# Two small layer-norm steps on GpSimd, a selector in another buffer, and a new instruction order in a four-layer graph network kernel

## The chip, the cores and the metric

The kernel runs on one core of one Trainium2 chip. The metric is the device time of one execution in microseconds (us), smaller is better. All executions quoted here are of the undisturbed, fast state. A comparison counts as faster or slower only from 2% on. TensorE is the matrix engine, VectorE, ScalarE and GpSimd are the elementwise engines, and in profile lines they are called PE (with PEld for its weight loads), DVE, ACT and POOL.

## The reference, cut to what matters

128 graphs of 64 nodes with 512 features each go through four layers. Each layer is `x = x + layer(relu(layernorm(x)), adj)`.

```python
def _layernorm(x, axis=-1, eps=1e-5):
    m = jnp.mean(x, axis=axis, keepdims=True)
    v = jnp.var(x, axis=axis, keepdims=True)
    return (x - m) / jnp.sqrt(v + eps)
# layer 0 on h = relu(layernorm(x)):
h = jax.nn.relu(hypergraph_conv(h, adj, W1, b1))     # 512 -> 1024
h = layer_norm(h, gamma, beta)
y = hypergraph_conv(h, adj, W2, b2)                  # 1024 -> 512, then + its input
# layer 1: s = (h @ w) @ a;  A = exp(leaky(8 tanh((s_i + s_j) / 8))) * adj, rows rescaled;  A @ h @ w
# layer 2: weight = adj * exp(q k^T), rows normalised;  weight @ value
# layer 3: attention from two vectors, then three powers of the transition with Wk[0..2], relu
# ... (inputs: x 128x64x512, adj 128x64x64, weights; all float32)
```

## The kernel before: the parts that matter

The program is a list of operations, each with an engine, an estimated cost and what it reads and writes. A list scheduler lays them out in one order per engine. The order depends on the estimated costs and on a table of start offsets (`AT`), stretches and periods. Every engine then executes its own instructions in that order, and an instruction whose input is late holds up the ones behind it (the timelines of VectorE and GpSimd below show it).

```python
class Graph:
    def op(self, eng, cost, fn, r=(), w=()):   # record one operation
        ...
    def run(self, slots, after):               # lay all out, by readiness, cost and priority, then emit
        ...

STRETCH, PERIOD1, PERIOD2 = (1.62, 0.5, 2.98, 1.93), 88.03, 82.78
AT = {
    "x0": -940.38, "apart": -46.64, "w1": -1103.01, "b1": -852.79, "w2": -823.68, ...   # start
    ... "m": 23.25, "h0": -18.86, "p0": 0.21, ... "y0": -114.53, ... "e0": -274.6, ...  # layers 0 and 1
    ... "hT": -11.06, "sh": 23.19, ... "b1_": 29.67,                                    # layers 2 and 3
}
```

The 128 graphs are 16 groups of 8. The first pass takes all groups through layers 0 and 1, the second through layers 2 and 3. One group takes some 74 us in either pass, and this is called a period below.

```python
def setup_l0():
    p, row, sel = Buf("ps"), Buf("o"), Buf("tmp")       # sel holds one of the four 128x512 temporaries
    for i in range(2):
        dve(0.2, lambda i=i: nc.vector.tensor_copy(quad(sel)[0:2, i, :], ...), [], [(sel, i)])
    # ... W2's row sums on TensorE, then spread over the partitions with the selector

def norm_stats(src, k, r):
    st, mv, ve, rs = Buf("st"), Buf("mv"), Buf("ve"), Buf("rs")
    for i in range(k):
        dve(0.69, lambda i=i: nc.vector.bn_stats(st.t[:, i, :], src(i)), [r[i]], [(st, i)])
    dve(0.19, lambda: nc.vector.bn_aggr(mv.t, ...), [...], [mv])
    dve(0.15, lambda: nc.vector.tensor_scalar_add(ve.t, mv.t[:, 1:2], EPS), [mv], [ve])
    pool(0.65, lambda: nc.gpsimd.tensor_tensor(rs.t, ve.t, mhalf, ALU.pow), [ve], [rs])
    return mv, rs

def pre_stats(g, t):
    mv, rs = norm_stats(...)
    dve(0.21, lambda: nc.vector.scalar_tensor_tensor(nm.t, mv.t[:, 0:1], -1.0, rs.t, op0=ALU.mult, op1=ALU.mult), [mv, rs], [nm])
    return nm, rs

def pre_ln(g, t, stats=None):        # h = relu(x * rstd - mean * rstd), on ScalarE
    ...

def layer0(g):
    ...
            h = pre_ln(g, t)
            pool(1.43, lambda xx=xx, h=h: nc.gpsimd.tensor_add(xx.t, xx.t, h.t), [h, xx], [xx])          # wide
            pool(1.39, lambda xx=xx: nc.gpsimd.tensor_add(xx.t, xx.t, b2_b.t), [xx, b2_b], [xx])         # wide
    ...     # W1 and W2 products as seven block products each; their input combinations on VectorE:
            #   dve(c_v(kc * P), lambda: nc.vector.tensor_tensor(d(), x_(), y_(), op), ...)
            # W2's results come out of PSUM on VectorE into y, and y into the output product:
            pe(c_mm(512, 1), lambda ...: nc.tensor.matmul(pf.t, M.t[:, t, :], y.t, start=True, stop=True), ...)

def layer1(g):
    ...
        h = pre_ln(g, t, stats[t])
        dot(lambda h=h: h.t, lambda: wa_b.t, ...)        # a dot product on VectorE, line 372
    ...
```

Of the kernel before, what the change touches and what calls it, by code (L numbers as in the profile page):

```python
# [11 lines left out]
ALU = mybir.AluOpType  # L12
AX = mybir.AxisListType

P = 128
# [6 lines left out]
EPS = 1e-5  # L22
# [139 lines left out]
def tile_adj_preln_d4(  # L162
# [6 lines left out]
    nc = tc.nc  # L169
# [74 lines left out]
    def c_mm(n, count):  # L244
        return 2 * count * max(n * 2 / 2400 + 0.0025, 0.111)
# [6 lines left out]
    def pe(cost, fn, r, w):  # L252
        return G.op("PE", cost, fn, r, w)

    def dve(cost, fn, r, w):
        return G.op("DVE", cost, fn, r, w)
# [4 lines left out]
    def pool(cost, fn, r, w):  # L261
        return G.op("POOL", cost, fn, r, w)
# [4 lines left out]
    def quad(b):  # L267
        return b.t.rearrange("p (c k) -> p c k", c=4)



    STRETCH, PERIOD1, PERIOD2 = (1.62, 0.5, 2.98, 1.93), 88.03, 82.78
    AT = {
        "x0": -940.38, "apart": -46.64, "w1": -1103.01, "b1": -852.79, "w2": -823.68, "w": 75.08, "c1": -847.71,
        "l0": -445.55, "c2": -663.72, "l1": 79.9, "c": -67.88, "g0": -1126.08, "g1": -1034.6, "g2": -833.84,
        "g3": -1004.6, "g": -1141.81, "l3": 18.25, "wg": 50.45, "w3": 213.12, "last": -71.37, "load1": -95.02,
        "load2": 65.29, "m": 23.25, "h0": -18.86, "p0": 0.21, "z0": 15.08, "q0": 10.02, "y0": -114.53, "h1": -19.75,
        "p1": -10.66, "z1": -12.15, "q1": -11.04, "y1": -111.67, "s": -30.12, "t0": 8.48, "e0": -274.6, "t1": 33.65,
        "e1": -92.85, "hT": -11.06, "sh": 23.19, "lq": 8.25, "pt": -36.14, "v": -8.42, "pv": -37.45, "s3": 0.07,
        "tt": -200.64, "a0": 29.6, "b0": -28.1, "a1": 61.9, "b1_": 29.67,  # L280
    }

    def part(name):
# [138 lines left out]
    def setup_l0():  # L422


        p, row, sel = Buf("ps"), Buf("o"), Buf("tmp")
        for i in range(2):
            dve(0.2, lambda i=i: nc.vector.tensor_copy(quad(sel)[0:2, i, :], ident[0:2, i:i + 1].to_broadcast([2, P])), [], [(sel, i)])
        gsc = const.tile([P, KH, 2], F32, name="gsc")
        dve(0.2, lambda: nc.vector.tensor_scalar(gsc[:, :, 0], gb2[:, 0, :], 1.0 / DH, None, op0=ALU.mult), ["gb2g"], ["gsc0"])
        dve(0.2, lambda: nc.vector.tensor_copy(gsc[:, :, 1], gb2[:, 1, :]), ["gb2b"], ["gsc1"])  # L430
# [4 lines left out]
        pe(c_mm(512, KH), mm, ["gsc0", "gsc1", *wkeys("w2", 0, KH)], [p])  # L435
        act(0.6, lambda: nc.scalar.copy(row.t[0:2, :], p.t[0:2, :]), [p], [row])
        pm, pb = Buf("ps"), Buf("ps")
        pe(c_mm(512, 1), lambda: nc.tensor.matmul(pm.t, quad(sel)[0:2, 0, :], row.t[0:2, :], start=True, stop=True), [row, (sel, 0)], [pm])
        pe(c_mm(512, 1), lambda: nc.tensor.matmul(pb.t, quad(sel)[0:2, 1, :], row.t[0:2, :], start=True, stop=True), [row, (sel, 1)], [pb])
        act(0.6, lambda: nc.scalar.copy(bw2_b.t, pb.t), [pb], [bw2_b])  # L440
        for c in range(KH):
            dve(0.75, lambda c=c: nc.vector.scalar_tensor_tensor(
# [59 lines left out]

    def norm_stats(src, k, r):

        st, mv, ve, rs = Buf("st"), Buf("mv"), Buf("ve"), Buf("rs")
        for i in range(k):
            dve(0.69, lambda i=i: nc.vector.bn_stats(st.t[:, i, :], src(i)), [r[i]], [(st, i)])  # L507
        dve(0.19, lambda: nc.vector.bn_aggr(mv.t, st.t[:, :k, :].rearrange("p k s -> p (k s)")), [(st, i) for i in range(k)], [mv])
        dve(0.15, lambda: nc.vector.tensor_scalar_add(ve.t, mv.t[:, 1:2], EPS), [mv], [ve])  # L509
        pool(0.65, lambda: nc.gpsimd.tensor_tensor(rs.t, ve.t, mhalf, ALU.pow), [ve], [rs])  # L510
        return mv, rs

    def pre_stats(g, t):

        xx, nm = xt[g, t], Buf("nm")
        mv, rs = norm_stats(lambda i: xx.t, 1, [xx])
        dve(0.21, lambda: nc.vector.scalar_tensor_tensor(nm.t, mv.t[:, 0:1], -1.0, rs.t, op0=ALU.mult, op1=ALU.mult), [mv, rs], [nm])  # L517
        return nm, rs

    def pre_ln(g, t, stats=None):  # L520
# [480 lines left out]
    for k in range(3):  # L1001
        src = Wk3[k].rearrange("(c p) o -> p c o", p=P)
        for c in (0, 2):
            i = k * KD + c
# [69 lines left out]
```

## Time and profile before

| | before |
|---|---|
| time, median (lowest to highest), 4 runs | 2438.2 us (2436.1 to 2440.3) |
| profiled span | 2439.8 us |
| first-pass period (mean between output products of the 5th and the 14th group) | 74.29 us |
| second-pass period | 73.81 us |

The engine shares, the stretches, the start and the groups are shown and read in the prediction. Two things are needed beside them.

A float32 matmul of the program stands in the trace as two records, and a transpose on TensorE as one (5933 matmuls and 64 transposes give the 11930 records). At full pace a record of 512 columns starts 0.43 us after the one before it. Ends of matmuls are modelled in this profile. So I also count TensorE's waits from start to start: the time from one matmul's start to the next one's, less what a matmul of its width takes at full pace. I did this count fully only after the prediction. The "waits" below are this count.

The chain of work that ended last, by engine, in the kernel before:

```profile
PE 71%; DVE 14%; DMA 7%; ACT 5%; issue 3%; SPq 0%; POOL 0%; DVEq 0%; ACTq 0%
```

TensorE was busy 98% of the time, but the chain that set the end was elsewhere for 29% of it, and nearly half of that is VectorE. TensorE's own instructions are therefore often released by something else at the last moment.

The timeline of the kernel before, at a place that comes back in every first-pass period (start, length, engine, line, operation; other lines between these are left out; L586 is a combination of the W1 product's inputs on VectorE, L695 and L696 are the wide additions of h and b2 on GpSimd, L594 is here a W1 product, L624 the last evacuation of a W2 product into y, L730 the output product that reads y):

```profile
556.83 1.27 POOL L695 TENSOR_TENSOR x<-x,h 128x512 f32<-128x512 f32 x1
557.07 1.31 DVE L586 TENSOR_TENSOR s_s_vu_tt<-mT_a 128x256 f32<-128x256 f32 x1
558.18 1.33 POOL L696 TENSOR_TENSOR x<-x,row_sh_q 128x512 f32<-128x512 f32 x1
558.42 1.37 DVE L586 TENSOR_TENSOR s_s_vu_tt<-s_s_vu_tt,mT_a 128x256 f32<-128x256 f32 x1
558.50 1.88 PE L594 MATMUL ps<-wa_mem,mT_a 128*128 128x512 f32 x4
...
559.71 0.41 DVE L586 TENSOR_TENSOR mT_a<-mT_a 128x256 f32<-128x256 f32 x1
560.04 0.41 DVE L624 TENSOR_TENSOR y_qT<-ps,u 128x256 f32<-128x256 f32 x1
...
560.51 1.12 PE L730 MATMUL ps<-y_qT,bd 128*128 128x512 f32 x2
```

Two combinations of 128x256 take 1.31 and 1.37 us beside GpSimd's wide additions, where the next one takes 0.41. Each ends 0.28 us after one of the additions (558.10 and 558.38, 559.51 and 559.79). The evacuation stands behind them in VectorE's queue, and the output product starts as soon as the evacuation ends (560.04 + 0.41 = 560.45). That is a wait of TensorE, though hardly any idle time shows for it.

This place is one of several. Of the 30.4 us of waits from 244 to 1160 us, 5.2 stand before output products. W1 products have 12.1, W2 products that read ScalarE's transposed copies (rT_a) 9.4, left multiplications 3.8.

### The profile page before, as it was taken

What the parts mean: (1) busy time and instruction counts of PE and PEld (TensorE: products, weight loads), DVE (VectorE), ACT (ScalarE), POOL (GpSimd) and SP (SyncE); (2) the same over time, 40 slices, a digit from 0 to 9 for tenths busy, and PEclk for the clock granted to TensorE, in tenths of its full rate; (3) what the DMA queues carried; (4) which work ended last, traced back from release to release, by engine and by line L of the source; (5) the groups of instructions that cost most, each with busy time, mean ns of one, the idle gap of its engine ahead of it and who ended that gap; (6) DMA issues with size and microseconds to landing.
All of it is one profiled execution on the core that took longest, in us unless ns stands there. A gap on an engine that the chain in (4) does not pass through costs nothing.

```text
span 2439.8 us, 33261 instructions
## 1 busy us (share of the span) xinstructions
PE 2381.8 (98%) x11930; PEld 1851.8 (76%) x11930; DVE 1836.4 (75%) x4252; ACT 1265.6 (52%) x1754; POOL 723.3 (30%) x874
## 2 busy tenths in 40 slices
PE   7999999999999999999999999999999999999999
PEld 3576667766667766677678888888888888888887
DVE  6888988888988889887778566666676766676764
ACT  2666565666555665555645455444455444454432
POOL 3233334333344323344223222222222222222221
PEclk8999999999999999999999999999999999999999
DMA  6322232222222322313453222223222223322211
GB/s 208 81 69 53 61 74 59 76 65 53 66 60 70 78 48 57 78 54 76 104 134 59 72 59 68 50 61 72 68 59 67 56 61 72 65 62 59 50 40 42
DMA packets 335927, 168.76 MB, mean 69 GB/s; under 512 B 284689, under 2 KB 290833, under 8 KB 335761
## 3 DMA queue, kind: packets, MB, share of 16 engines
q1 hardware_dynamic: 335760, 166.63, 28.2%
q8 instruction: 94, 1.54, 0.3%
q14 instruction: 73, 0.59, 0.1%
HBM read 64.76 MB, written 34.70 MB: 41 GB/s over the span
## 4 chain that ended last, share of the span: by engine, by line
PE 71%; DVE 14%; DMA 7%; ACT 5%; issue 3%; SPq 0%; POOL 0%; DVEq 0%; ACTq 0%
PE ps L594 48%; PE ps L817 12%; PE ps L533 3%; DMA z_hT<-tmp_mB_s 3%; PE ps L935 2%; DVE s_s_vu_tt L586 2%; DVE st L507 2%; PE ps L878 2%; DMA rw<-row 1%; PE ps L730 1%; DVE nm L517 1%; ACT h L524 1%; ACT rT_a L544 1%; DVE s_s_vu_tt L868 1%; DVE x L731 1%
## 5 line engine op out<-in xcount | busy, mean ns | idle before, releaser
L524 ACT ACTIVATE h<-x,nm,rs 128x512 f32<-128x512 f32 x384 | 303.1, 811 | 541.3 <-DVE nm L517 490.2
L594 PE MATMUL ps<-wb_mem,rT_a 128*128 128x256 f32 x2056 | 477.9, 381 | 10.3 <-ACT rT_a L544 8.4
L594 PEld LDWEIGHTS ps<-wb_mem,rT_a 128*128 128x128 f32 x2056 | 387.2, 190 | 78.1 <-ACT rT_a L544 20.5
L510 POOL TENSOR_TENSOR rs<-ve,mhalf 128x1 f32<-128x1 f32 x320 | 199.2, 624 | 692.6 <-DVE ve L509 605.6
L594 PE MATMUL ps<-wb_mem,s_s_vu_tt 128*128 128x256 f32 x1152 | 275.0, 380 | 0.6 <-DVE s_s_vu_tt L586 0.6
L594 PE MATMUL ps<-wb_mem,tmp_mB_s 128*128 128x256 f32 x1152 | 261.6, 379 | 1.0 <-DVE tmp_mB_s L586 1.0
L594 PE MATMUL ps<-wa_mem,mT_a 128*128 128x512 f32 x512 | 243.0, 603 | 9.3 <-ACT u L562 7.4
L594 PE MATMUL ps<-wb_mem,mT_a 128*128 128x256 f32 x1016 | 242.7, 380 | 0.0
L594 PEld LDWEIGHTS ps<-wb_mem,tmp_mB_s 128*128 128x128 f32 x1152 | 217.5, 190 | 30.8 <-DVE tmp_mB_s L586 1.8
L594 PEld LDWEIGHTS ps<-wb_mem,s_s_vu_tt 128*128 128x128 f32 x1152 | 216.3, 190 | 31.8 <-DVE s_s_vu_tt L586 2.0
L594 PEld LDWEIGHTS ps<-wb_mem,mT_a 128*128 128x128 f32 x1016 | 189.8, 190 | 30.5 <-issue 6.0
L507 DVE BATCH_NORM_STATS2 st<-x 128x6 f32<-128x512 f32 x256 | 175.9, 687 | 28.0 <-DMA x<-xm 25.3
L594 PEld LDWEIGHTS ps<-wa_mem,mT_a 128*128 128x128 f32 x512 | 93.8, 191 | 123.8 <-issue 95.7
L948 POOL TENSOR_TENSOR u<-u,bk_b 128x256 f32<-128x256 f32 x96 | 75.7, 796 | 368.6 <-DVE x L953 215.2
L594 PE MATMUL ps<-wa_mem,s_s_vu_tt 128*128 128x512 f32 x384 | 183.0, 600 | 1.3 <-DVE z_hT L614 1.3
L562 ACT COPY u<-ps 128x256 f32<-128x256 f32 (+1 forms) x160 | 73.0, 456 | 200.0 <-PE ps L594 153.6
L544 ACT COPY rT_a<-z_hT 128x1024 uint16<-128x1024 uint16 x128 | 145.4, 1160 | 21.6 <-DMA z_hT<-tmp_mB_s 21.4
L564 DVE TENSOR_TENSOR u<-ps,u 128x256 f32<-128x256 f32 (+1 forms) x160 | 84.5, 528 | 95.6 <-PE ps L594 64.2
L533 PEld LDWEIGHTS ps<-bd,h 128*128 128x128 f32 x1024 | 129.0, 193 | 33.6 <-issue 13.6
L695 POOL TENSOR_TENSOR x<-x,h 128x512 f32<-128x512 f32 x64 | 86.2, 1346 | 194.0 <-ACT h L524 194.0
L952 DVE TENSOR_TENSOR u<-ps,u 128x256 f32<-128x256 f32 x96 | 40.6, 423 | 136.3 <-PE ps L594 121.6
L533 PE MATMUL ps<-bd,h 128*128 128x128 f32 x1024 | 132.2, 278 | 3.6 <-DVE bd L759 1.5
(172 smaller groups left out, 4248.4 us busy)
## 6 DMA issues: line engine op xcount, KB each, us to landing
x<-in_x_dram SPq DMA_DIRECT2D x64, 256.0 KB, 2.7
xm<-x SPq DMA_DIRECT2D x64, 256.0 KB, 2.0
x<-xm SPq DMA_DIRECT2D x64, 256.0 KB, 2.6
out_dram<-x SPq DMA_DIRECT2D x64, 256.0 KB, 2.2
adj<-in_adj_dram SPq DMA_DIRECT2D x32, 256.0 KB, 4.2
rw<-row SPq DMA_DIRECT2D x96, 64.0 KB, 3.2
wb_mem<-in_Wk_dram SPq DMA_DIRECT2D x6, 512.0 KB, 4.8
wa_mem<-in_W1T_dram SPq DMA_DIRECT2D x2, 1024.0 KB, 8.5
```

The lines of the kernel that those rows point to most:

```text
L507: dve(0.69, lambda i=i: nc.vector.bn_stats(st.t[:, i, :], src(i)), [r[i]], [(st, i)])
L510: pool(0.65, lambda: nc.gpsimd.tensor_tensor(rs.t, ve.t, mhalf, ALU.pow), [ve], [rs])
L524: act(0.82, lambda: nc.scalar.activation(h.t, xx.t, AF.Relu, bias=nm.t, scale=rs.t), [xx, nm, rs], [h])
L533: nc.tensor.matmul(quad(p)[:, c, :], h.t[:, c * P:(c + 1) * P], rhs(), start=True, stop=True)
L544: act(1.16, lambda: nc.scalar.copy(u16(dst()).rearrange("p c (k q) -> p c k q", q=2), u16(back()).rearrange("p (q c r) -> p c r q", q=2, c ...
L562: act(n / 1200 + 0.17, lambda: nc.scalar.copy(at(0)(), p1.t[:, :n]), [p1], [(U, 0)])
L564: dve(c_v(n), lambda: nc.vector.tensor_add(at(1)(), p2.t[:, :n], at(0)()), [p2, (U, 0)], [(U, 1)])
L586: dve(c_v(kc * P), lambda: nc.vector.tensor_tensor(d(), x_(), y_(), op), [*kx, *ky], kd)
L594: nc.tensor.matmul(p.t[:, :n], lhs()[:, c, :], rhs(c), start=first and c == 0, stop=c == kc - 1, skip_group_check=True)
L695: pool(1.43, lambda xx=xx, h=h: nc.gpsimd.tensor_add(xx.t, xx.t, h.t), [h, xx], [xx])
L817: nc.tensor.matmul(pair(p.t)[:, o, :], a, b, start=first and o == 0 and c == 0, stop=c == 1, skip_group_check=True)
L948: pool(0.88, lambda: nc.gpsimd.tensor_add(U.t[:, iv], U.t[:, u[1]], add()), [u, ka], [v])
```

## The change

The intent: take two one-column steps of every layer norm off VectorE, give the start one more temporary, and lay the order out anew for the new costs.

```diff
-    STRETCH, PERIOD1, PERIOD2 = (1.62, 0.5, 2.98, 1.93), 88.03, 82.78
+    STRETCH, PERIOD1, PERIOD2 = (2.01, 1.52, 3.8, 3.15), 99.32, 100.99
     AT = {
-        "x0": -940.38, ... "m": 23.25, "h0": -18.86, ... "y0": -114.53, ... "e0": -274.6, ...
+        "x0": -1000.31, ... "m": -52.0, "h0": -37.33, ... "y0": -29.58, ... "e0": -103.04, ...
     ...   (all entries of the table are new)
-        p, row, sel = Buf("ps"), Buf("o"), Buf("tmp")
+        p, row, sel = Buf("ps"), Buf("o"), Buf("rw")
     ...   (and the views of sel to match)
-        dve(0.15, lambda: nc.vector.tensor_scalar_add(ve.t, mv.t[:, 1:2], EPS), [mv], [ve])
-        pool(0.65, lambda: nc.gpsimd.tensor_tensor(rs.t, ve.t, mhalf, ALU.pow), [ve], [rs])
+        pool(0.3, lambda: nc.gpsimd.tensor_scalar_add(rs.t, mv.t[:, 1:2], EPS), [mv], [rs])
+        pool(0.65, lambda: nc.gpsimd.tensor_tensor(rs.t, rs.t, mhalf, ALU.pow), [rs], [rs])
     ...
-        dve(0.21, lambda: nc.vector.scalar_tensor_tensor(nm.t, mv.t[:, 0:1], -1.0, rs.t, op0=ALU.mult, op1=ALU.mult), [mv, rs], [nm])
+        pool(0.3, lambda: nc.gpsimd.tensor_scalar(nm.t, mv.t[:, 0:1], rs.t, -1.0, op0=ALU.mult, op1=ALU.mult), [mv, rs], [nm])
```

## The prediction

> **What bounds the kernel now.** I read the page's engine shares first, then busy time by stretch, then the start on the TensorE timeline, then the groups by form for every operation that the change touches.
>
> The page, by engine:
> ```profile
> PE 2381.8 (98%) x11930; PEld 1851.8 (76%) x11930; DVE 1836.4 (75%) x4252; ACT 1265.6 (52%) x1754; POOL 723.3 (30%) x874
> ```
> TensorE is busy 98% of 2439.8 us, so it sits idle for only 58.0 us. All of VectorE, ScalarE and GpSimd lies beside it. A shorter small operation on those engines is worth only what it takes away from TensorE's waits.
>
> Where those 58 us lie: busy us of each engine by stretch (columns: stretch, length, then PE, PEld, DVE, ACT, POOL busy, granted clock, DMA share, GB/s):
> ```profile
> 0.00:61.00 61.00, 44.50 (x124) 21.39 (x125) 39.78 (x82) 13.09 (x20) 22.40 (x29) 0.89 0.62 208
> ...
> 244.00:1160.00 916.00, 903.02 (x3754) 640.76 (x3753) 781.70 (x1816) 534.39 (x756) 348.64 (x403) 1.00 0.27 65
> ...
> 1400.00:2380.00 980.00, 970.61 (x5780) 832.84 (x5778) 656.39 (x1526) 459.02 (x623) 229.34 (x291) 1.00 0.27 60
> ```
> The start (0 to 61 us) has 61.00 - 44.50 = 16.5 us of idle, the steady first pass (layers 0 and 1) 13.0 us in 916, the steady second pass 9.4 us in 980. The rest, some 19 us, is the end of the setup (5 us), the passage between the two passes (9 us) and the tail (5 us). VectorE has 85% in the first pass (781.70 of 916): it is the engine next to the bound there, and it has 67% in the second.
>
> The start on TensorE's timeline (start, length, work; in brackets the idle before it and what ended it):
> ```profile
> 5.59 5.45 PE L468 MATMUL ps<-tmp_mB_s 128*128 128x512 f32 x8 [5.59 <-DMA tmp_mB_s<-in_Wk_dram]
> 15.53 3.29 PE L468 MATMUL ps<-tmp_mB_s 128*128 128x512 f32 x4 [4.49 <-DMA tmp_mB_s<-in_Wk_dram]
> ...
> 44.20 3.78 PE L594 MATMUL ps<-wa_mem,mT_a 128*128 128x512 f32 x4 [3.21 <-ACT u L562]
> 47.77 3.06 PE L594 MATMUL ps<-wa_mem,s_s_vu_tt 128*128 128x512 f32 x4
> 50.67 7.03 PE L468 MATMUL ps<-tmp_mB_s 128*128 128x512 f32 x16
> ```
> The 512-wide matmul takes 7.03 / 16 = 0.44 us at 50.67 but 3.78 / 4 = 0.94 us at 44.20, just after an idle stretch. So an idle stretch of TensorE at the start is paid twice. Taking 0.43 us as the full pace, the cold matmuls at 5.59, 15.53, 44.20 and 47.77 cost about 2.0 + 1.6 + 2.1 + 1.3 = 7 us more. Start waste: about 16.5 + 7 = 23.5 us.
>
> **What the Trainium skill says.** "TensorE: Matmul & The Clock Gate", Part 1, What's actually happening: TensorE runs at half clock until it has been busy for about 3.4 us, and falls back after an idle window of that length. The trace agrees (0.94 against 0.44 us, above). "Perfetto Trace Analysis", Identifying the Most-Contended Engine: matmul occupancy is not the distance from the roofline, weight-load busy share is better; here 76%. "SBUF — State Buffer", Practical consequences: a VectorE instruction with two SBUF inputs contends with a GpSimd instruction that reads SBUF. The trace has such spreads (the 128x1 product of line 517 has a median of 152 ns and a longest of 1266 ns). "GPSIMD Engine Reference", 3.1: GpSimd pays a larger dispatch and more cycles per element than VectorE; the rows below agree.
>
> **The change part by part.** The groups by form (count, busy us, mean ns, idle before and its cause):
> ```profile
> L509 DVE TENSOR_SCALAR ve<-mv 128x1 f32<-128x1 f32 x320 | 49.0, 153 | 10.3
> L517 DVE SCALAR_TENSOR_TENSOR nm<-mv,rs 128x1 f32<-128x1 f32 x256 | 58.0, 232 | 22.8 <-POOL rs L510 22.3 <-POOL s_s_vu_tt L858 0.3
> ...
> L510 POOL TENSOR_TENSOR rs<-ve,mhalf 128x1 f32<-128x1 f32 x320 | 199.2, 624 | 692.6 <-DVE ve L509 605.6 <-DVE nm L517 58.3 <-ACT rT_a L939 16.8
> ...
> L695 POOL TENSOR_TENSOR x<-x,h 128x512 f32<-128x512 f32 x64 | 86.2, 1346 | 194.0 <-ACT h L524 194.0
> ...
> L948 POOL TENSOR_TENSOR u<-u,bk_b 128x256 f32<-128x256 f32 x96 | 75.7, 796 | 368.6 <-DVE x L953 215.2 <-DVE u L566 152.0
> ```
> *Layer norm steps.* Removed from VectorE: 320 additions of eps at 153 ns = 49.0 us, and 256 products -mean * rstd at 232 ns = 58.0 us (the rows give the busy sums; records overlap slightly). Together 107 us, so VectorE falls from 1836 to about 1729 us, 71%. Added to GpSimd: the same 576 instructions. The fixed cost, an estimate from the rows: 128x512 takes 1346 and 128x256 takes 796, so 256 elements cost 550 ns and nothing costs about 246 ns. 576 x 0.25 = 144 us, so GpSimd goes from 723 to about 867 us, 36%. The chain bn_aggr, eps, power, product, activation loses one hand-over (VectorE to GpSimd to VectorE to ScalarE becomes VectorE to GpSimd to ScalarE), and the product no longer queues behind wide VectorE work; it gains about 0.2 us of slower arithmetic. What ends TensorE's waits in the first pass is instead the evacuations and the transposed copies (line 624 before line 730, 566 and 562 before the next W1 product, 544 before the W2 product): a layer norm does not appear among them, it is computed far ahead. So 107 us off VectorE is worth little directly: I put 2 us on it, for evacuations that find VectorE free.
>
> *Selector.* The two 2x128 copies move from one of the four temporaries to the row buffer, which nobody uses until the first attention row. In the kernel before, the selector held a temporary from 1.8 to about 41 us, so the four Wq, Wk pairs had three buffers: the second Wk is issued at 11.08, only after the first pair's matmuls, and lands at 15.40, and the fourth pair is only multiplied at 50.67. In the new order, both first pairs can be issued at once.
>
> *Order.* The instruction order of the new kernel (built, not run) has the same 5997 matmuls. The DMA queue starts with the 2 MB of W1, then two Wq, Wk pairs, then four x tiles, then adj. From the landings before, the stream goes at 0.65 us per 256 KB after some 3 us, so 3 MB land by about 10 us: TensorE starts near 9.5 instead of 5.6 (4 us later), but then runs both pairs without the 4.5 us hole, until about 20. The small products and two left multiplications follow at 20 to 25.5 (24.6 to 30.2 before), then pairs 3 and 4 (16 matmuls at 0.43 plus the bias columns, 8.7 us), then the W2 row sums (7.0 us), to about 41. Before, at 44.2, TensorE had done the same but for pairs 3 and 4 (8.7 us), and had done a W1 product and the two selector products (4 us). So the new one is 3.2 + 8.7 - 4 = about 8 us ahead, and runs warm where the old one paid 3.4 us at 44 to 50. I count 8 in all, as evacuations may open a hole of their own.
> In the steady first pass, the old period of about 74 us has some 2 us of waits of 0.1 to 0.6 us, repeated 16 times. The new period still puts a W2 product, one W1 product (0.86 us) and the output product together once, as before, but the second time a left multiplication and a W1 product more stand between them; W2 products come in runs of 12 and 16. I count 0.3 us per period, 5 us. In the second pass the weight loads and matmuls leave almost nothing: 0. The passage and tail: 0, give or take 3.
>
> Sum: 2439 - 2 - 8 - 5 = 2424 us.
>
> **Rivals.** (1) GpSimd becomes slow to deliver: three dependent small steps, queued behind 1.35 us additions in order, delay the activations. For: the power already takes 624 ns, and GpSimd and VectorE share reads. Against: 45% of GpSimd at most in the first pass, and layer norm lies ahead of need. If it did, every group would lose about 1 us, +30: 2455 to 2470. (2) The new order loses in the steady passes what it wins at the start: a hole of 0.5 us more in each of 32 periods is 16 us, so 2445. For: the order was made with a model of costs, not on this trace. (3) VectorE was the hidden limit of the first pass, and its relief removes all waits there: another 20 us, 2404. Against: TensorE's idle there is only 13 us. (4) Transfers hidden anyway: if the x tiles and not Wk limit the start, the selector brings nothing and W1 first costs 4 us: 2434.
>
> **Range and chances.** 2% is 49 us. All idle is 58 us and the cold clock 7, of which at least 10 us of the start (first weights) and the tail can't go; so faster by over 2% would need nearly everything. 2% slower would need rival 1 in full in every period. Range 2404 (rival 3) to 2443 (near rival 2).
>
> **What would show it.** Right: VectorE busy near 1730 and GpSimd near 865; TensorE busy in the first 61 us up from 44.5 to 49 or more, with the first matmul near 9.5 us and no second hole before 19; the first pass period down by some 0.3 us; the second pass equal. Wrong if activations of h end TensorE's waits, if the small GpSimd steps take over 0.4 us, or if a transition between passes opens several us.

## The result, and the profile after

| | before | after |
|---|---|---|
| median, 4 runs each | 2438.2 us | 2399.9 us (2397.0 to 2403.2) |
| ratio, 95% interval | | 0.9843 (0.9826 to 0.9860) |
| profiled span | 2439.8 us | 2395.1 us |
| first-pass period | 74.29 us | 71.77 us |
| second-pass period | 73.81 us | 73.21 us |
| first matmul starts at | 5.6 us | 9.5 us |
| waits of TensorE from there to 61 us | 20.1 us | 8.5 us |
| waits in 61 to 122 us | 3.2 us | 6.2 us |
| waits in 244 to 1160 us | 30.4 us | 2.6 us |

Here and below, a ratio is the mean time of one kernel's fast runs over that of the other kernel's fast runs of the same rounds, so it isn't quite the ratio of the medians. By the 2% rule the two kernels are the same. The time came out 24 us under the one predicted, and 4 us under the predicted range.

The page of the changed kernel, by engine:

```profile
PE 2356.3 (98%) x11930; PEld 1855.0 (77%) x11930; DVE 1721.2 (72%) x3676; ACT 1263.5 (53%) x1754; POOL 938.2 (39%) x1450
```

TensorE is still at 98%. This number, at which one would look first, says nothing about what happened. VectorE lost 115 us, GpSimd gained 215 us.

The chain that ended last, by engine, in the changed kernel:

```profile
PE 84%; DVE 6%; DMA 4%; ACT 2%; POOL 2%; issue 2%; SPq 0%; DVEq 0%; POOLq 0%; ACTq 0%
```

This line does say it: the chain runs on TensorE itself for 84% instead of 71%, and VectorE's part fell from 14% to 6%.

Busy time by stretch in the changed kernel (columns as in the prediction):

```profile
0.00:61.00 61.00, 48.81 (x170) 24.96 (x171) 44.55 (x84) 16.52 (x26) 36.66 (x54) 0.97 0.69 237
244.00:1160.00 916.00, 914.62 (x3858) 661.74 (x3857) 725.82 (x1605) 555.01 (x786) 429.62 (x665) 1.00 0.27 68
```

In the first pass TensorE's idle time fell from 13.0 to 1.4 us, and it ran 3858 matmul records in the 916 us instead of 3754. That is 2.8% more work in the same time, far more than 11.6 us of idle explain; the waits between starts explain it. The weight loads show it too: their busy time in this stretch rose from 640.76 to 661.74 us, by 3.3%, where groups came 3.5% faster.

The start of the changed kernel on TensorE's timeline:

```profile
9.52 8.34 PE L469 MATMUL ps<-tmp_mB_s 128*128 128x512 f32 x12 [9.52 <-DMA tmp_mB_s<-in_Wk_dram]
...
23.34 2.02 PE L534 MATMUL ps<-bd,h 128*128 128x128 f32 x16 [1.14 <-ACT bd L682]
26.21 7.10 PE L469 MATMUL ps<-tmp_mB_s 128*128 128x512 f32 x16 [0.84 <-DMA tmp_mB_s<-in_Wk_dram]
...
34.92 7.03 PE L435 MATMUL ps<-wb_mem,gsc 128*2 128x512 f32 x16
```

TensorE starts 3.9 us later than before, then runs to 44 us with no idle hole above 1.14 us. All four weight pairs are done at 33 us; before, the last pair was still running at 57 us.

The groups by form of the moved steps in the changed kernel (count, busy us, mean ns, idle before and its cause):

```profile
L518 POOL TENSOR_SCALAR nm<-mv,rs 128x1 f32<-128x1 f32 x256 | 119.3, 466 | 26.4
L510 POOL TENSOR_SCALAR rs<-mv 128x1 f32<-128x1 f32 x320 | 101.5, 317 | 534.2 <-DVE mv L509 452.9 <-ACT rT_a L940 43.7 <-ACT mT_a L940 16.7
```

The two steps take 317 and 466 ns on average on GpSimd where I had estimated 250, 221 us in all instead of 144. Their medians in the trace are 222 and 265 ns, and the longest 839 and 1383: most take about what was estimated, and the mean is made by those that are held up (three in ten take over 1.3 times the median). What holds them up is not in these rows.

One group of the W1 combinations on VectorE, first in the kernel before, then in the changed kernel:

```profile
L586 DVE TENSOR_TENSOR s_s_vu_tt<-s_s_vu_tt,mT_a 128x256 f32<-128x256 f32 x64 | 40.8, 638 | 2.0
```

```profile
L587 DVE TENSOR_TENSOR s_s_vu_tt<-s_s_vu_tt,mT_a 128x256 f32<-128x256 f32 x64 | 27.1, 423 | 1.7
```

The same instruction takes 423 ns instead of 638 on average, and at most 426 instead of 1376: in the new order none of them is held up. Not every group does so well: the one before it in the queue fell from 638 to 514 ns, and in f2 (below), with the same period, this one takes 505.

The place of the output product in the changed kernel's timeline (L625 is the evacuation, L595 a W1 product, L731 the output product):

```profile
581.49 0.81 DVE L625 TENSOR_TENSOR y_qT<-ps,u 128x256 f32<-128x256 f32 x2
581.61 1.88 PE L595 MATMUL ps<-wa_mem,mT_a 128*128 128x512 f32 x4
...
583.33 1.88 PE L731 MATMUL ps<-y_qT,bd 128*128 128x512 f32 x4
```

The evacuation ends at 582.30 and the output product comes at 583.33: a full microsecond of slack where before there was none. A W1 product keeps TensorE busy meanwhile, but one stood there before too (558.50). What changed is VectorE's queue: no slowed combinations stand in front of the evacuation.

The two profiled executions are 44.7 us apart. Counted from the span's start, so with the wait for the first matmul, the waits differ by stretch as follows: 0 to 61 us, 7.7 us fewer (11.6 fewer after the first matmul, which comes 3.9 later); 61 to 122, 3.0 more; 122 to 244, 4.2 fewer; 244 to 1160, 27.8 fewer; 1160 to 1400, the passage between the passes, under 1 fewer; from 1400 us on some 7 fewer (6 to 7, as one takes the full pace of the smallest matmuls). Together that is the 44.7 us to within 0.5.

### The profile page after: what moved, and what is told of

Its sections match the earlier page's. It is cut to its first block, busy times and chain, and to the rows that moved or that the text cites. A ratio compares the mean times of both kernels' runs of the same rounds, so it can differ in the third digit from the quotient of the medians.

```text
span 2395.1 us, 33543 instructions
## 1 busy us (share of the span) xinstructions
PE 2356.3 (98%) x11930; PEld 1855.0 (77%) x11930; DVE 1721.2 (72%) x3676; ACT 1263.5 (53%) x1754; POOL 938.2 (39%) x1450
## 4 chain that ended last, share of the span: by engine, by line
PE 84%; DVE 6%; DMA 4%; ACT 2%; POOL 2%; issue 2%; SPq 0%; DVEq 0%; POOLq 0%; ACTq 0%
PE ps L595 60%; PE ps L818 11%; PE ps L534 4%; PE ps L936 2%; PE ps L731 2%; PE ps L879 2%; DVE s_s_vu_tt L869 1%; DMA x<-xm 1%; PE ps L844 1%; ACT o L543 1%; DVE bd L854 1%; ACT h L525 1%; POOL u L867 1%; POOL rs L511 1%; DVE st L508 1%
## 5 line engine op out<-in xcount | busy, mean ns | idle before, releaser
L595 PE MATMUL ps<-wb_mem,rT_a 128*128 128x256 f32 x2056 | 476.8, 380 | 1.7 <-DVE z_hT L615 0.9
L595 PEld LDWEIGHTS ps<-wb_mem,rT_a 128*128 128x128 f32 x2056 | 386.5, 190 | 74.8 <-issue 20.3
L510 POOL TENSOR_SCALAR rs<-mv 128x1 f32<-128x1 f32 x320 | 101.5, 317 | 534.2 <-DVE mv L509 452.9
L595 PE MATMUL ps<-wb_mem,s_s_vu_tt 128*128 128x256 f32 x1152 | 275.0, 379 | 0.2 <-DVE s_s_vu_tt L587 0.2
L595 PE MATMUL ps<-wb_mem,tmp_mB_s 128*128 128x256 f32 x1152 | 261.3, 379 | 0.2 <-DVE tmp_mB_s L587 0.2
L595 PEld LDWEIGHTS ps<-wb_mem,s_s_vu_tt 128*128 128x128 f32 x1152 | 218.5, 190 | 43.1 <-issue 10.5
L595 PE MATMUL ps<-wb_mem,mT_a 128*128 128x256 f32 x1016 | 240.7, 380 | 1.8 <-ACT u L563 1.3
L595 PEld LDWEIGHTS ps<-wb_mem,tmp_mB_s 128*128 128x128 f32 x1152 | 217.6, 190 | 29.6 <-DVE tmp_mB_s L587 0.6
L595 PE MATMUL ps<-wa_mem,mT_a 128*128 128x512 f32 x512 | 238.0, 593 | 2.1 <-DVE u L567 2.1
L511 POOL TENSOR_TENSOR rs<-rs,mhalf 128x1 f32<-128x1 f32 x320 | 202.9, 634 | 26.6
L595 PEld LDWEIGHTS ps<-wb_mem,mT_a 128*128 128x128 f32 x1016 | 190.6, 190 | 28.6 <-ACT u L563 1.5
L595 PE MATMUL ps<-wa_mem,s_s_vu_tt 128*128 128x512 f32 x384 | 182.9, 599 | 1.0 <-ACT c_b L453 0.6
L595 PEld LDWEIGHTS ps<-wa_mem,mT_a 128*128 128x128 f32 x512 | 96.0, 190 | 105.4 <-issue 92.5
L623 POOL TENSOR_TENSOR u<-u,row_sh_q 128x256 f32<-128x256 f32 x96 | 70.9, 746 | 235.0 <-DVE u L565 205.9
L707 ACT ACTIVATE z_hT<-z_hT 128x512 f32<-128x512 f32 x128 | 79.8, 625 | 116.7 <-DVE z_hT L615 116.6
```

The costliest lines, as they stand in the source:

```text
L510: pool(0.3, lambda: nc.gpsimd.tensor_scalar_add(rs.t, mv.t[:, 1:2], EPS), [mv], [rs])
L511: pool(0.65, lambda: nc.gpsimd.tensor_tensor(rs.t, rs.t, mhalf, ALU.pow), [rs], [rs])
L595: nc.tensor.matmul(p.t[:, :n], lhs()[:, c, :], rhs(c), start=first and c == 0, stop=c == kc - 1, skip_group_check=True)
L707: act(0.63, lambda: nc.scalar.activation(z.t[:, cols], z.t[:, cols], AF.Relu), [(z, j)], [(z, j)])
```

## The experiments

My theory after reading the two traces was **order**: the new order alone lets TensorE run the first pass without waits, and where the small steps run matters little. The rival was **relief**: VectorE was the hidden limit of the first pass, and 107 us less of its work removed the waits. This is the third rival of the prediction. All times below are medians, the ratios are against the kernel before in the same rounds. The kernel before had medians of 2435.1, 2436.1, 2436.3, 2441.1 and 2441.8 us in the five sets of runs, each on another chip, so medians of different sets agree only within some 5 us and ratios are the better measure between sets.

| run | what it is | median us | ratio (95%) | first-pass period us |
|---|---|---|---|---|
| f1_old_order_gpsimd | old order, both steps on GpSimd | 2479.6 | 1.0182 (1.0167 to 1.0197) | 76.84 |
| f2_new_order_vector | new order, both steps on VectorE | 2402.3 | 0.9865 (0.9850 to 0.9879) | 71.77 |
| e1_norm_only | before plus moved steps, scheduled anew | 2494.8 | 1.0243 (1.0227 to 1.0258) | 77.12 |
| e2_order_only | before plus all new constants | 2450.7 | 1.0057 (1.0040 to 1.0074) | 74.55 |
| h1_old_start | after, old start constants | 2414.3 | 0.9913 (0.9896 to 0.9929) | 71.77 |
| h2_old_first_pass | after, old first-pass constants | 2497.3 | 1.0252 (1.0237 to 1.0268) | 77.08 |
| h3_old_second_pass | after, old second-pass constants | 2413.1 | 0.9904 (0.9888 to 0.9921) | 71.77 |
| e3_no_selector | after, selector in a temporary | 2404.9 | 0.9872 (0.9858 to 0.9887) | 71.77 |
| h5_b_new_first | before, new first-pass constants | 2417.3 | 0.9923 (0.9908 to 0.9938) | 71.77 |
| g1_no_b2 | before without the b2 additions | 2420.1 | 0.9933 (0.9918 to 0.9948) | 72.96 |
| f3_old_order_eps | old order, eps on GpSimd | 2449.7 | 1.0055 (1.0040 to 1.0070) | 75.37 |
| f4_old_order_product | old order, product on GpSimd | 2451.3 | 1.0059 (1.0042 to 1.0076) | 75.20 |
| f5_f1_no_b2 | f1 without the b2 additions | 2447.3 | 1.0028 (1.0017 to 1.0039) | 74.42 |
| d1_f2_more_vector | f2 with more work on VectorE | 2439.9 | 0.9997 (0.9988 to 1.0006) | 73.37 |
| g2_no_adds | before without both wide additions | 2418.1 | 0.9902 (0.9887 to 0.9917) | 72.89 |
| f6_f1_no_adds | f1 without both wide additions | 2432.8 | 0.9960 (0.9945 to 0.9975) | 73.26 |
| k1_product_vector | after, product on VectorE | 2397.1 | 0.9813 (0.9799 to 0.9828) | 71.77 |
| k2_eps_vector | after, eps on VectorE | 2398.9 | 0.9826 (0.9809 to 0.9842) | 71.77 |

Where differences of less than 2% are read as differences here, it is because the 95% intervals of the ratios lie apart. All gave a correct result except g2_no_adds and f6_f1_no_adds, which leave out an addition on purpose. (b2 is all zeros in these inputs, so leaving its addition out changes no result here.) By the 2% rule e1 and h2 are slower than the kernel before, k1 is unclear, and all others are the same.

Several expectations missed. f1 (2479.6) is above every case that was written down, and e1 and h2 are above theirs by 35 and 7 us. f3, f5 and h3 fell between their two cases. h5 is 2 us above its range, e2 and k1 are within 1 us outside. h1 had 13.7 us of waits in its first 61 us where 16 to 20 were expected, and g1's period fell by 1.33 us where 0.4 to 1 was. f2's VectorE was 1789 us busy, not near 1830.

### The order and the small steps, crossed

The scheduler's order depends on the engine and cost that an operation is recorded with. To keep an order exactly, the two crossed kernels keep the recorded engine and cost and change only which engine's instruction is emitted.

f1_old_order_gpsimd, from the kernel before:

```diff
-        dve(0.15, lambda: nc.vector.tensor_scalar_add(ve.t, mv.t[:, 1:2], EPS), [mv], [ve])
-        pool(0.65, lambda: nc.gpsimd.tensor_tensor(rs.t, ve.t, mhalf, ALU.pow), [ve], [rs])
+        dve(0.15, lambda: None, [mv], [ve])
+        def eps_pow():
+            nc.gpsimd.tensor_scalar_add(ve.t, mv.t[:, 1:2], EPS)
+            nc.gpsimd.tensor_tensor(rs.t, ve.t, mhalf, ALU.pow)
+        pool(0.65, eps_pow, [ve, mv], [rs])
...
-        dve(0.21, lambda: nc.vector.scalar_tensor_tensor(nm.t, ...), [mv, rs], [nm])
+        dve(0.21, lambda: nc.gpsimd.tensor_scalar(nm.t, mv.t[:, 0:1], rs.t, -1.0, op0=ALU.mult, op1=ALU.mult), [mv, rs], [nm])
```

> The order of the kernel before, matmul for matmul and operation for operation, but eps and -mean * rstd are emitted on GpSimd at the same places. Order theory (the new order alone took the first pass's waits away): the first-pass period stays near 74 us and the time at 2432 to 2440. Relief theory (VectorE's 107 us less is what took them away): the period falls to about 72 us and the time to about 2405 to 2412. Half and half: near 2420.

f2_new_order_vector, from the changed kernel:

```diff
-        pool(0.3, lambda: nc.gpsimd.tensor_scalar_add(rs.t, mv.t[:, 1:2], EPS), [mv], [rs])
+        pool(0.3, lambda: nc.vector.tensor_scalar_add(rs.t, mv.t[:, 1:2], EPS), [mv], [rs])
...
-        pool(0.3, lambda: nc.gpsimd.tensor_scalar(nm.t, ...), [mv, rs], [nm])
+        pool(0.3, lambda: nc.vector.scalar_tensor_tensor(nm.t, mv.t[:, 0:1], -1.0, rs.t, op0=ALU.mult, op1=ALU.mult), [mv, rs], [nm])
```

> The order of the changed kernel, matmul for matmul, but the two small steps are emitted on VectorE at the places where GpSimd had them. Order theory: the period stays at 71.8 us and the time at 2398 to 2405, with VectorE back near 1830 us busy. Relief theory: the period goes back to about 74 us, the time to about 2430.

Measured: f1 took 2479.6 us, 44 us more than before, and f2 took 2402.3, 33 us less than before. The stretch from 400 to 1000 us decides it. Busy time by engine in it (PE, PEld, DVE, ACT, POOL), for the kernel before:

```profile
400.00:1000.00 600.00, 591.54 (x2463) 420.07 (x2462) 512.83 (x1197) 354.51 (x501) 225.52 (x262) 1.00 0.27 66
```

for f1:

```profile
400.00:1000.00 600.00, 573.49 (x2368) 402.22 (x2367) 473.11 (x996) 339.36 (x482) 265.31 (x411) 1.00 0.25 61
```

for f2:

```profile
400.00:1000.00 600.00, 600.00 (x2526) 432.69 (x2525) 505.81 (x1231) 360.80 (x516) 243.84 (x272) 1.00 0.26 66
```

and for the changed kernel:

```profile
400.00:1000.00 600.00, 600.00 (x2525) 432.50 (x2524) 476.53 (x1057) 368.32 (x522) 281.69 (x436) 1.00 0.26 66
```

f1 has VectorE relieved (473 instead of 513 us busy), and TensorE gets less done (2368 records instead of 2463). f2 has VectorE nearly as loaded as before (506 us), and TensorE is busy for all 600 us with 2526 records, as many as the changed kernel. So the order carries the gain and the relief does not; f2 shows it directly. f1 is not relief alone, as it loads GpSimd too, and relief alone in the old order was not run. The first-pass period is 71.77 us in f2 as in the changed kernel, to the hundredth: with 1.1 and 2.6 us of waits in the 916 us from 244 on, that is TensorE's own pace for a group.

What the moved steps are worth in the new order is at the edge of what the runs tell: f2 and the changed kernel differ by 2.3 us in the medians and by 0.0022 in the ratio (some 5 us), with overlapping intervals.

### The parts as a scheduler user would try them

e1_norm_only has the new `norm_stats` and `pre_stats` of the diff above with the old constants; e2_order_only has all the new constants and nothing else.

```diff
 # e2_order_only, from the kernel before
-    STRETCH, PERIOD1, PERIOD2 = (1.62, 0.5, 2.98, 1.93), 88.03, 82.78
+    STRETCH, PERIOD1, PERIOD2 = (2.01, 1.52, 3.8, 3.15), 99.32, 100.99
     ... (and the new table)
```

> The kernel before with the new norm_stats and pre_stats alone; the constants of the order are the old ones, so that the scheduler lays out another order from the new costs (its matmul order shows no short repeating period). Order theory: constants that were fitted to other costs give an order no better than before, 2430 to 2460. Relief theory: 2405 to 2420.

> The kernel before with the new constants alone; norm steps on VectorE, selector in the temporaries. Order theory in its plain form (the constants carry the gain): 2400 to 2410. If the constants fit only the costs that they were found with: 2420 to 2450, as the first pass finds no short period. Relief theory: about 2430.

Measured: 2494.8 and 2450.7 us, both longer than before. These are not clean halves, as another engine, cost or constant gives another order. e2's period stays at 74.55 us, although f2 shows that an order with the small steps on VectorE can reach 71.77. It isn't the recorded costs that keep e2 there: h5 below has the same ones, only without the new start and second-pass constants, and reaches 71.77. Why e2 doesn't is not shown. What follows is only that neither e1 nor e2 gains.

### Which part of the order

Three kernels put back one part of the old constants, one puts back the selector's buffer, and one gives the kernel before only the new first-pass constants.

```diff
 # h1_old_start, from the changed kernel: the table's start entries
-        "x0": -1000.31, "apart": -0.04, "w1": -1140.59, ...
+        "x0": -940.38, "apart": -46.64, "w1": -1103.01, ...
```

```diff
 # h2_old_first_pass, from the changed kernel: entries of layers 0 and 1
-    STRETCH, PERIOD1, PERIOD2 = (2.01, 1.52, 3.8, 3.15), 99.32, 100.99
+    STRETCH, PERIOD1, PERIOD2 = (1.62, 0.5, 3.8, 3.15), 88.03, 100.99
     ... "load1": -95.02, "m": 23.25, ... "e1": -92.85
```

```diff
 # h3_old_second_pass, from the changed kernel: entries of layers 2 and 3
+    STRETCH, PERIOD1, PERIOD2 = (2.01, 1.52, 2.98, 1.93), 99.32, 82.78
     ... "wg": 50.45, ... "hT": -11.06, ... "b1_": 29.67
```

```diff
 # h5_b_new_first, from the kernel before: the new entries of layers 0 and 1
+    STRETCH, PERIOD1, PERIOD2 = (2.01, 1.52, 2.98, 1.93), 99.32, 82.78
     ... "load1": -120.84, "m": -52.0, ... "e1": -32.68
```

```diff
 # e3_no_selector, from the changed kernel (with the views to match)
-        p, row, sel = Buf("ps"), Buf("o"), Buf("rw")
+        p, row, sel = Buf("ps"), Buf("o"), Buf("tmp")
```

> The changed kernel with the old constants for the setup and first loads alone; after three groups its matmul order settles on the same period as the changed kernel's. If the first pass is worth about 30 us and the start about 10: the time is 2408 to 2415, the first 61 us have about 16 to 20 us of waits, the steady period 71.8 us. If the start were the larger part of the gain: 2425 or more.

> The changed kernel with the old constants of layers 0 and 1 alone (start and second pass new, small steps on GpSimd). If the first pass's order carries the gain, and GpSimd's steps cost in an order that was not fitted to them: a period of 74 to 77 us, 2440 to 2490. If GpSimd's relief carried it: near 2405.

> The changed kernel with the old constants of layers 2 and 3 alone. The second pass had only some 6 us less waiting after the change: 2400 to 2410. If the second pass and the passage between the passes mattered more than the traces say: 2415 or more.

> The kernel before (small steps on VectorE, selector in the temporaries, old start, old second pass) with the new constants of layers 0 and 1 alone. Its matmul order settles on a short period of its own that is like the changed kernel's. If longer runs between producer and use are what takes the waits away: a first-pass period of 71.8 to 72.3 us, the time 2405 to 2415. If the exact order of the changed kernel is needed: 2425 to 2445.

> The changed kernel with the selector back in a temporary. Only the start can differ, as the steady period of its matmul order is the same: 4 to 10 us slower, 2404 to 2410, the first 61 us with a hole that waits for the second or third Wk. If the selector was worth nothing once W1 is loaded first: within 2 us of the changed kernel.

Measured: the old first-pass constants undo everything and more (2497.3 us, period 77.08; like e1, an old-constant order with the steps recorded on GpSimd). The new first-pass constants alone, in the kernel before with its small steps on VectorE, reach the period of 71.77 us and take 19 us off (2417.3). So the first pass is where the larger part lies. Putting back the old start costs 14 us by the medians (2414.3), the old second pass 13 us (2413.1, with a wide spread from 2407 to 2417), and the selector in a temporary 5 us (2404.9). Those three are differences of medians between sets of runs, so good to about 5 us, and the selector's is not resolved.

The traces do not put these losses into the first 61 us. h1 has 13.7 us of waits to 61 us after its first matmul, instead of 8.5, but that matmul comes 2.4 us earlier, and by 122 us h1 is only 1.5 us behind. It loses 8 us from 122 to 244 us, while its order settles on the period, and some 4 each in the rest of the first pass and in the passage. In e3 TensorE waits 1.93 us at 18.79 for a Wk, as expected, and has 13.2 us of waits to 61 us. But f2, k1 and k2, which share the changed kernel's order, have 9.7, 11.7 and 7.2 there, and by 122 us e3 is level with the changed kernel (24.5 and 24.2 us from the span's start). So what the selector is worth is not shown.

### Why the moved steps cost 44 us in the old order

This is a second question: the prediction had said that these steps lie far ahead of need. Either step alone first, in the exact old order, each with its half of f1's edit:

```diff
 # f3_old_order_eps (VectorE's eps emits nothing)
+        pool(0.65, lambda: (nc.gpsimd.tensor_scalar_add(ve.t, ...), nc.gpsimd.tensor_tensor(rs.t, ve.t, mhalf, ALU.pow)), [ve, mv], [rs])
 # f4_old_order_product
+        dve(0.21, lambda: nc.gpsimd.tensor_scalar(nm.t, mv.t[:, 0:1], rs.t, -1.0, ...), [mv, rs], [nm])
```

> The old order exactly, only the addition of eps on GpSimd. With both steps on GpSimd it took 44 us more. If the product -mean * rstd is what hurts (its place in GpSimd's queue is behind two wide additions, and the activation, the dot product and VectorE's queue wait for it): 2433 to 2445 here. If the longer chain before the power hurts: 2455 or more.

> The old order exactly, only the product -mean * rstd on GpSimd. If it stands in GpSimd's queue behind the wide additions and delays the activations: 2460 to 2480, nearly all of the 44 us. If the two steps share the cost: 2450 to 2460. If eps hurts: 2433 to 2445.

Measured: 2449.7 and 2451.3 us, 13 and 15 us over the kernel before in the same rounds. Together they cost 44, more than the sum. The trace of f1 shows a path. Its timeline at one tile of layer 1 (other lines between these are left out; L512 is eps, L513 the power, L521 the product, L528 the activation of h, L372 VectorE's dot product with h):

```profile
556.46 0.22 POOL L512 TENSOR_SCALAR ve<-mv 128x1 f32<-128x1 f32 x1
556.76 0.57 POOL L513 TENSOR_TENSOR rs<-ve,mhalf 128x1 f32<-128x1 f32 x1
557.30 0.22 POOL L512 TENSOR_SCALAR ve<-mv 128x1 f32<-128x1 f32 x1
557.61 0.57 POOL L513 TENSOR_TENSOR rs<-ve,mhalf 128x1 f32<-128x1 f32 x1
558.28 0.27 POOL L521 TENSOR_SCALAR nm<-mv,rs 128x1 f32<-128x1 f32 x1
...
558.58 2.93 ACT L528 ACTIVATE h<-x,nm,rs 128x512 f32<-128x512 f32 x4 [5.93 <-POOL nm L521]
...
559.43 0.69 DVE L372 SCALAR_TENSOR_TENSOR o<-h,row_sh_q 128x512 f32<-128x512 f32 x1 [1.08 <-ACT h L528]
```

By the order of the records, the first tile's product stands on GpSimd behind the second tile's eps and power, the activation waits for it, and VectorE stands still for 1.08 us at its dot product with everything behind it held up. How often VectorE waits there, from the waits by cause (us in total, times, longest us), in the kernel before:

```profile
DVE o L372 <- ACT h L524: 2.9, 4, 0.9
```

in f1:

```profile
DVE o L372 <- ACT h L528: 77.1, 83, 2.4
```

and in the changed kernel:

```profile
DVE o L372 <- ACT h L525: 18.0, 28, 1.6
```

The changed kernel has some of it too, but its evacuations have slack (above), so TensorE doesn't feel it.

This path belongs to the product. f4, with the product alone moved, has 30.0 us of this wait. f3, with eps alone, has 3.2, hardly more than the 2.9 before, and still loses 13 us. There VectorE waits more in front of its own product, for GpSimd's power; that this makes f3's loss is likely and not shown. First the kernel before, then f3:

```profile
DVE nm L517 <- POOL rs L510: 22.3, 43, 0.7
```

```profile
DVE nm L517 <- POOL rs L510: 57.2, 117, 1.2
```

The next four runs ask whether GpSimd's wide additions are what makes it so costly. g1 and f5 leave out the addition of b2, g2 and f6 both wide additions of layer 0; g1 and g2 have the small steps on VectorE, f5 and f6 on GpSimd. All have the exact old order.

```diff
 # g1_no_b2 from the kernel before, f5_f1_no_b2 from f1
-                pool(1.39, lambda xx=xx: nc.gpsimd.tensor_add(xx.t, xx.t, b2_b.t), [xx, b2_b], [xx])
+                pool(1.39, lambda: None, [xx, b2_b], [xx])
 # g2_no_adds from the kernel before, f6_f1_no_adds from f1: as above, and
-                pool(1.43, lambda xx=xx, h=h: nc.gpsimd.tensor_add(xx.t, xx.t, h.t), [h, xx], [xx])
+                pool(1.43, lambda: None, [h, xx], [xx])
```

> The kernel before in its exact order, without the 64 GpSimd additions of b2 (zeros in these inputs, so the result stays right). In the old order, VectorE's two-input combinations run at 1.3 us instead of 0.42 beside those additions, ahead of the evacuation that the output product waits for. If that contention makes the waits of the first pass: some 0.4 to 1 us less per period, 2420 to 2430. If the waits are of the order alone: within 3 us of the kernel before.

> Both small steps on GpSimd in the old order, as in f1_old_order_gpsimd (2480 us), without the 64 wide additions of b2 (zeros, the result stays right). If f1 lost 44 us because the small steps queue behind GpSimd's wide additions and hold up activations, and VectorE's dot products behind those: most of the 44 us goes, 2420 to 2435, VectorE's wait for h in front of the dot products falls from 77 us to under 20. If the loss is the longer arithmetic of the chain itself: 2455 to 2470 (only the 16 us that the additions cost in the old order anyway).

> The kernel before in its exact order, without both wide GpSimd additions of layer 0 (x + h and x + b2, 64 each of 128x512). Leaving out x + h makes the result wrong on purpose. It is the base for the run with the same additions left out and the small steps on GpSimd. Without the b2 additions alone it was 2420 us. Both theories: 2405 to 2420, as VectorE's two-input operations then meet fewer GpSimd instructions.

> The old order with both small steps on GpSimd, without both wide additions of layer 0 (wrong on purpose). Theory queue (the small steps cost what they do because they stand behind 1.3 us additions on GpSimd): the loss against the same kernel with the small steps on VectorE shrinks from 27 us (b2 additions out) to 12 or less, and the VectorE dot products' wait for the activation falls from 57.5 to under 25 us. Rival chain (three dependent small GpSimd instructions, each with its own start and hand-over, are late even on an empty GpSimd): the loss stays at 20 us or more and the wait above 45 us.

Measured, as the loss from moving the small steps:

| | period, VectorE | period, GpSimd | loss per period | difference of ratios |
|---|---|---|---|---|
| all wide additions (before, f1) | 74.29 | 76.84 | 2.55 us | 0.0182 |
| without b2 (g1, f5) | 72.96 | 74.42 | 1.46 us | 0.0095 |
| without both (g2, f6) | 72.89 | 73.26 | 0.37 us | 0.0058 |

The loss per period of the first pass falls to a seventh as the wide additions go. So those additions are what makes the moved steps costly there. What remains, 14.7 us by the medians, lies for some 5.6 us before the last output product and for the rest after it: layers 2 and 3 have the moved steps too, and their own GpSimd work was left in. My expectation for f5 was missed: 2447.3 us is not in 2420 to 2435, and the dot products' wait fell to 57.5 us, not under 20. That for f6 was half missed: 14.7 us is neither under 12 nor over 20, and the dot products' wait fell only to 44.5 us in f6, where I had put it under 25:

```profile
DVE o L372 <- ACT h L528: 44.5, 59, 2.4
```

So that wait is not a measure of the loss: more than half of it stays while the first-pass loss nearly goes. Two things happen when the wide additions go, and these runs don't part them: the small steps wait less on GpSimd, and VectorE has more slack (g2 has it 486 us busy of the 600, before 513), so that the same wait does less harm. How much each is worth stays open. g1 alone also shows what the b2 additions cost before any step was moved: 64 of them fewer, with VectorE's program untouched, make the period 1.33 us shorter. The combination of the rows above falls from 638 to 430 ns, and the waits from 244 to 1160 us from 30.4 to 15.1 us, those before output products to nothing. The 12 us before W2 products and left multiplications stay; they go in the new order (h5 has 0.7 us of waits in all from 244 to 1160 us).

### Is VectorE's load indifferent in the new order?

d1_f2_more_vector takes f2 and does every `bn_aggr` three times on VectorE, some 4.5 us of extra work per group in the first pass.

```diff
 # d1_f2_more_vector, from f2
-        dve(0.19, lambda: nc.vector.bn_aggr(mv.t, ...), ...)
+        dve(0.19, lambda: [nc.vector.bn_aggr(mv.t, ...) for _ in range(3)], ...)
```

> The new order with the small steps on VectorE, as in f2_new_order_vector (2402 us), and each statistics aggregate done three times: 12 x 2 x 0.19 = 4.5 us more VectorE work per group of the first pass, over 90% of its period. If the new order leaves VectorE slack at every evacuation: the period stays at 71.8 to 72.3 us and the time at 2400 to 2415. If VectorE's load at f2's level was just at the edge: 73 to 76 us, 2425 to 2470.

Measured: 2439.9 us, a period of 73.37 us, TensorE 591 us busy of the 600. So the new order has room for f2's load on VectorE but not for 4.5 us more: VectorE's load is not indifferent, it is just inside what this order hides. (The extra aggregates also delay the power by some 0.4 us; load and delay were not parted.) "Order, not relief" holds for the step from before to after, not for any load.

### Mixtures in the new order

```diff
 # k1_product_vector, from the changed kernel: only the product back on VectorE
+        pool(0.3, lambda: nc.vector.scalar_tensor_tensor(nm.t, mv.t[:, 0:1], -1.0, rs.t, op0=ALU.mult, op1=ALU.mult), [mv, rs], [nm])
 # k2_eps_vector, from the changed kernel: only eps back on VectorE
+        pool(0.3, lambda: nc.vector.tensor_scalar_add(rs.t, mv.t[:, 1:2], EPS), [mv], [rs])
```

> The changed kernel's exact order with eps on GpSimd and the product -mean * rstd on VectorE. With both on GpSimd it is 2399.9, with both on VectorE 2402.3. Theory order: anywhere from 2398 to 2404, the placement hardly matters there; the dot products' wait for the activation falls from 18 to under 8 us. Rival relief (VectorE's load sets the time): 2401 to 2402, between the two.

> The changed kernel's exact order with eps on VectorE and the product on GpSimd. Theory order: 2398 to 2404 again. If either of these mixtures is under 2396 it beats both kernels.

Measured: 2397.1 and 2398.9 us, both with the period of 71.77. The dot products' wait fell to 1.5 us in k1 as expected, and its time hardly moved. Neither came under the 2396 that I had set for beating both kernels. k1's ratio of 0.9813 against the changed kernel's 0.9843, from another set of runs, has an interval that touches the other's, so a lead of k1 by some us is possible and not shown. In the new order the placement of these two steps is worth a few us at most.

## Why the prediction was wrong

That the change stays within 2% held; the time did not: 2399.9 us against 2424, and just outside 2404 to 2443. By the prediction's steps:

- **The first pass.** The step that failed is "I count 0.3 us per period, 5 us". The period fell by 2.52 us, and the waits from 244 to 1160 us from 30.4 to 2.6 us. I had written down "some 2 us of waits" per period, which is nearly the whole of them (2.5), so the size of what could be won was known. What failed is the step from there to 0.3: that the new order keeps the wait of the output product "as before". I had looked only at the order of the matmuls. One W1 product does stand in front of the output product in both kernels, and it takes 1.72 us and not 0.86. But the wait came from VectorE's queue, where the evacuation stood behind combinations slowed to 1.3 us, and there the new order leaves a full microsecond of slack. The waits of the W2 products for ScalarE's copies, 9.4 us, went too; I had named them and expected nothing of them. Against rival 3 I also measured the room by idle time, "TensorE's idle there is only 13 us". The term should have been the whole wait, about 2.5 us per period.
- **The start.** Predicted 8 us ahead. At 61 us it was 7.7 (11.6 us fewer waits, a first matmul 3.9 us later); by 122 us 3.0 of that had come back, so 4.7 stays. The first matmul at 9.52 was predicted at 9.5, TensorE's 48.81 us busy of the first 61 at 49 or more, and there was no second hole before 19 us.
- **The small steps on VectorE.** 2 us were put on the relief. f2 against the changed kernel gives 2.3 us by the medians, some 5 by the ratios. The size stands as far as it is resolved. VectorE's busy time came out at 1721 for 1729, partly by luck: 48 us of its fall come with the order alone (1836 to 1789 in f2), and the moved steps take 68 more, not 107.
- **The small steps on GpSimd.** 144 us were estimated and 221 measured; the estimate of 250 ns fits the medians (222 and 265 ns), not the means, because some run longer (a product up to 1.38 us). The busy time of GpSimd was 938 instead of 867 us, and my sign of being wrong ("over 0.4 us") was met by the product. In the new order it cost no time that these runs resolve.
- **The second pass.** Predicted 0, measured 6 to 7 us in the trace; restoring the old constants there costs 13 us by the medians. A smaller miss in the same direction.
- **"It is computed far ahead"**, of the layer norm, is not supported by f1: in the old order the same move cost 44 us. Rival 1 (GpSimd slow to deliver, 2455 to 2470) describes what the moved steps do without the new order, and f1's 2480 is even beyond it.
- **Rival 3** named the size (2404, another 20 us) by luck, with the wrong cause: f1 has the relief and is slower, f2 lacks the relief and is as fast.
- **Rivals 2 and 4** did not happen: the new order did not lose in the steady passes, and the time of 2434 did not come. Whether the selector's buffer brings anything, which rival 4 doubts, is not resolved (e3).

What the Trainium skill gave: "TensorE: Matmul & The Clock Gate" (Part 1) and the cold start held, the granted clock in the first 61 us rose from 0.89 to 0.97. "Perfetto Trace Analysis", Tensor Engine Instruction, says that the end of a matmul is estimated from its size and not observed. I had not used this, and it is the reason for counting starts and not busy time. The same page, Identifying the Most-Contended Engine, recommends the weight-load share over matmul busy time. I cited it and then did not use it: between the two kernels that share rose in the first pass by 3.3% with the pace, where matmul busy time rose by 1.3%. The same page, Optimizing Scalar/DVE Operations, warns that moving operations between VectorE and GpSimd "might not help", as they share a port; f1 (44 us slower) and f2 (2 to 5 us apart) agree.

## What to carry to other kernels

When an engine is 98% busy, take the room for a gain from start to start or from the chain that ended last, not from idle time: here idle said 13 us, starts said 30, and 28 of them went. Judge an order and a move of instructions apart, by keeping the recorded order and changing only the emitted engine; re-running a scheduler with half of the change tests something else. A small step moved to another in-order queue costs what it makes the next queue wait for, and that depends on the order: the same move cost 44 us in one order and no time that these runs resolve in another.

## What the Trainium skill lacked or had wrong

- "GPSIMD Engine Reference", 3.1, gives per-element rates and a measured wide addition but no time for a one-column instruction. Here a 128x1 addition took 317 ns and a 128x1 product with a per-partition scalar 466 ns on average (medians 222 and 265 ns), a 128x1 power 634 ns; on VectorE the same two steps took 153 and 232 ns.
- "SBUF — State Buffer", Who interferes with whom, describes the shared pair as an exclusive lock, and the timeline agrees: both slowed combinations end 0.28 us after a GpSimd addition. It quotes slowdowns of 6.8 and 1.5 times from other measurements, none for this pair: a 128x256 combination took 1.31 to 1.37 us beside a wide GpSimd addition and 0.41 us without, and 64 wide additions fewer on GpSimd made a period 1.33 us shorter with VectorE's program untouched.
- No page that I read has the cost of a small step at the head of another engine's in-order queue: the same 576 instructions moved to GpSimd cost 44 us in the old order and none that these runs resolve in the new.
